# Layer 1 of a two-layer convolution kernel: one product for three taps, row shifts by DMA, and normalisation moved to ScalarE

## The chip, the cores and the metric

The kernel runs on one core of one Trainium2 chip. The metric is the device time of one execution in microseconds (us), lower is better. All data is float32. The engines are TensorE (PE in the profile, with PEld for its weight loads), VectorE (DVE), ScalarE (ACT), GpSimd (POOL) and SyncE (SP), which only issues DMAs here.

## The reference, cut to what matters

The input x has 2 images of 128 channels, 256 rows and 256 columns. Layer 0 is a group norm, a windowed attention with halo and a residual sum; its result goes to memory. The change concerns layer 1 (a further group norm `_gn` and a residual sum stand around this function):

```python
t1 = conv(x, w1, padding=((2, 2), (0, 0)))                    # 128 -> 128 channels, 5 taps down the rows
t3 = conv(t1, w3, padding=((1, 1), (0, 0)), feature_group_count=c)   # 3 taps down the rows, each channel alone
xp = pad(x, 2 columns left and right)
t2 = stack([xp[..., 0:w], xp[..., 2:w + 2], xp[..., 4:w + 4]])  # three taps along a row, 2 columns apart
t4 = einsum('nckhw,ckg->nghw', t2, w4[:, :, 0, :])             # 128 channels x 3 taps -> 8 channels
t5 = t4[:, None] * t3.reshape(n, c // g, g, h, w)              # the 8 channels multiply all 16 groups of t3
```

The output is `x + t5`, with x the input of the layer. The "unfolded products" are t4.

## The kernel before, in words

Channels lie on the 128 partitions. Both layers go through an image in strips of 8 rows, 32 strips per image, 64 strips in all. Layer 0 (`attention_fast`) writes its result x1 to memory; layer 1 (`convolutions_fast`) reads it back, 8 rows at a time, and a function per step issues the instructions. The order on each engine is the order in which the code calls these functions (`manual_schedule` over all five engines): an engine never takes a later instruction first.

One strip k of layer 1 in the order of the loop:

- `load_rows1(k + 2)`, L636 and L638: two DMAs of SP bring the rows of the strip after next into `raw` (six buffers).
- `unfold(k)`, L692: 12 matmuls into the PSUM tile `g`: for each of 3 taps, one for each of 4 pairs of rows. The weight is 128 x 32, its 8 real columns padded with zeros to 32; row pair j goes to PSUM partitions 32j to 32j + 31. ScalarE copies `g` to `t4` (L698).
- `first_rows(k)`, L723: ScalarE copies two rows of the vertical convolution from the strip before.
- `start_strip(k + 1)`, which is `normalise1`: ScalarE copies four rows of `xm` (the normalised input `xn`) from the strip before (L649), then VectorE subtracts the mean and multiplies by `rstd`, 128 x 2048 elements (L651).
- `vertical(k, 2)`: the 5-tap convolution for four rows, in PSUM tiles `a_c`, `a_d`, `a_e`, `a_o` (L706 and L740), in this order on TensorE, taken in turn from three buffers. ScalarE copies `a_c` to `both` (L737); VectorE forms `c` (L744) and the even and odd rows of `t1` (L751, L757); ScalarE starts `t3` (L762).
- `row_sums(k + 1)`: ScalarE copies one row of `sm` (L677), VectorE forms sums and differences of rows, `sm` and `df` (L678, L682), for the next strip.
- `depthwise(k, 2)`: VectorE, two instructions on `t3` (L769). Then `vertical(k, 4)` for the other four rows.
- `spread(k)`, L780: four matmuls with the selection matrix `sel` copy the 8 channels of `t4` to all 128 partitions, into the PSUM tiles `b`. `combine` multiplies them by `t3` (L789), with `depthwise(k, 4)` between its halves.
- `finish(k)`: a GpSimd DMA adds x1 from memory to `y` (L797), then an SP DMA writes `y` out (L798).

Group-norm values come from `Norms.steps`, whose small instructions are spread over several strips.

Of the kernel before, what the change touches and what calls it, by code (L numbers as in the profile page):

```python
# [9 lines left out]
F32 = mybir.dt.float32  # L10
I32 = mybir.dt.int32
AF = mybir.ActivationFunctionType
# [33 lines left out]

def host_constants():
    ident = np.eye(P, dtype=np.float32)  # L50
    gavg = np.zeros((P, P), np.float32)
    for g in range(P // 4):
        gavg[4 * g : 4 * g + 4, 4 * g : 4 * g + 4] = 0.25

    kb = np.zeros((HEADS, 32, 6, 10), np.float32)
    for c in range(10):
        kb[:, c, :, c] = 1.0
    for r in range(6):
        kb[:, 10 + r, r, :] = 1.0
    kb[:, 16, :, 6:] = NEG  # L60
    kb[:, 17, :, :4] = NEG
    flag = np.zeros((2, 4 * NPAIR * 4, 2, 4), np.float32)
    flag[0, :, 0] = 1.0
    flag[1, :, 1] = 1.0


    hot = np.zeros((2, HEADS, 16, 2, 64), np.float32)
    for key in range(64):
        j, i = divmod(key, 6)
        for e in range(2):  # L70
            if 0 <= j - 4 * e < 6:
                hot[:, :, j - 4 * e, e, key] = 1.0
            else:
                hot[:, :, 12, e, key] = NEG
            if key < 60:
                hot[:, :, 6 + i, e, key] = 1.0


    keep = np.zeros((2, HEADS, 16, 2, 2), np.float32)
    for i in range(2):  # L80
        keep[:, i::2, 0:12, i, 0] = 1.0
        keep[:, i::2, 12, i, 1] = 1.0

    sel = np.zeros((4, 32, P), np.float32)
    for ch in range(P):
        sel[:, ch % 8, ch] = 1.0
    return {
        "c_ident": ident,
        "c_sel": sel.reshape(P, P),
        "c_gavg": gavg,  # L90
        "c_kb": kb.reshape(P, 60),
        "c_flag": flag.reshape(2, 4 * NPAIR, 32),
        "c_hot": hot.reshape(P, 128),
        "c_keep": keep.reshape(P, 4),
        "c_head": np.stack([(np.arange(P) // DH % 2 == i) for i in range(2)], 1).astype(np.float32),
    }


class Norms:
# [15 lines left out]
    def steps(self, st, ps_pool, name, tag="pj"):  # L115

        nc, glob, small, gavg = self.nc, self.glob, self.small, self.gavg
        mv = small.tile([P, 2], F32, tag="mv", name=f"mv_{name}")
        nc.vector.bn_aggr(mv, st.rearrange("p n k -> p (n k)"))
        yield  # L120
        pm = ps_pool.tile([P, 512], F32, tag=tag, name=f"pm_{name}")
        nc.tensor.matmul(pm[:, 0:1], gavg, mv[:, 0:1], start=True, stop=True)
        yield
        mean = glob.tile([P, 1], F32, tag=f"mean_{name}", name=f"mean_{name}")
        nc.vector.tensor_copy(mean, pm[:, 0:1])
        d = small.tile([P, 1], F32, tag="d", name=f"d_{name}")
        nc.vector.tensor_sub(d, mv[:, 0:1], mean)
        q = small.tile([P, 1], F32, tag="q", name=f"q_{name}")
        nc.vector.tensor_mul(q, d, d)
        nc.vector.tensor_add(q, q, mv[:, 1:2])  # L130
        yield
        pv = ps_pool.tile([P, 512], F32, tag=tag, name=f"pv_{name}")
        nc.tensor.matmul(pv[:, 0:1], gavg, q, start=True, stop=True)
        yield
        v = small.tile([P, 1], F32, tag="v", name=f"v_{name}")
        nc.vector.tensor_scalar(v, pv[:, 0:1], 1e-5, None, ALU.add)
        yield
        sd = small.tile([P, 1], F32, tag="sd", name=f"sd_{name}")
        nc.scalar.activation(sd, v, AF.Sqrt)
        yield  # L140

        r0 = small.tile([P, 1], F32, tag="r0", name=f"r0_{name}")
        nc.vector.reciprocal(r0, sd)
        nc.vector.tensor_mul(r0, r0, v)
        nc.vector.tensor_add(r0, r0, sd)
        nc.vector.tensor_scalar(r0, r0, 0.5, None, ALU.mult)
        rstd = glob.tile([P, 1], F32, tag=f"rstd_{name}", name=f"rstd_{name}")
        nc.vector.reciprocal(rstd, r0)
        self.done[name] = mean, rstd
        yield  # L150

    def group(self, st, ps_pool, name):
        for _ in self.steps(st, ps_pool, name):
            pass
        return self.done[name]


def attention_fast(tc, io, x1_d, norm, st_x, st_y, tags, ends, weights):
# [6 lines left out]
    with ExitStack() as l0:  # L165
# [120 lines left out]
        def normalise(k):  # L286
            b, s = divmod(k, NS)
            if s == 0:
                norms[b] = norm.group(st_x[b], ps_pj, f"x{b}") if b == 0 else norm.done[f"x{b}"]
                st_y[b] = norm.new(f"st_y{b}", tags[(2 * b + 2) % 3])  # L290
                if b + 1 < NB:
                    st_x[b + 1] = norm.new(f"st_x{b + 1}", tags[(2 * b + 1) % 3])
# [290 lines left out]
class Weights:  # L583


    def __init__(self, nc, io, glob):
        self.nc, self.io = nc, io
        self.w1 = glob.tile([P, 5, P], F32, tag="w1", name="w1")
        self.w3 = glob.tile([P, 3], F32, tag="w3", name="w3")
        self.w4 = glob.tile([P, 3, 32], F32, tag="w4", name="w4")  # L590
        self.sel = glob.tile([P, P], F32, tag="sel", name="sel")
        self.w1s = glob.tile([P, 6, P], F32, tag="w1s", name="w1s")

# [13 lines left out]
def convolutions_fast(tc, io, x1_d, norm, st_y, out, weights, count_good):  # L607
# [4 lines left out]
    with ExitStack() as l1:  # L612
# [25 lines left out]
                nc.sync.dma_start(t[:, 5:8, :], x1_d[b][s + 1][:, 0:3, :])  # L638
            raws[b, s] = t

        def normalise1(b, s, k, mean, rstd):
            cur, prev = xn[k % 2], xn[(k + 1) % 2]
            if s == 0:
                nc.gpsimd.memset(cur[:, 0:1, :], 0.0)
                nc.vector.tensor_scalar(
                    cur[:, 1:4, 2 : 2 + W], raws[b, -1][:, 5:8, :], mean, rstd, ALU.subtract, ALU.mult
                )
            else:
                nc.scalar.copy(cur[:, 0:4, :], prev[:, 8:12, :])  # L649
            n = 8 if s + 1 < NS else 5  # L650
            nc.vector.tensor_scalar(  # L651
                cur[:, 4 : 4 + n, 2 : 2 + W], raws[b, s][:, 0:n, :], mean, rstd, ALU.subtract, ALU.mult
            )
            if n < 8:
                nc.gpsimd.memset(cur[:, 4 + n : 12, :], 0.0)

        t1s, sms, dfs = {}, {}, {}

# [25 lines left out]
        def unfold(k):  # L686

            xt = xn[k % 2]
            pg = ps_pj.tile([P, 512], F32, tag="pj", name=f"g_{k}")
            for tap in range(3):  # L690
                for j in range(4):
                    nc.tensor.matmul(  # L692
                        pg[32 * j : 32 * j + 32, :], w4[:, tap, :],
                        xt[:, 2 * j + 1 : 2 * j + 3, 2 * tap : 2 * tap + W],
                        start=tap == 0, stop=tap == 2,
                    )
            t4 = wk.tile([P, 512], F32, tag="t4", name=f"t4_{k}")
            nc.scalar.copy(t4, pg)  # L698
            t3 = wk.tile([P, 8, W], F32, tag="t3", name=f"t3_{k}")
            y = wk.tile([P, 8, W], F32, tag="y", name=f"y_{k}")  # L700
            ts[k] = t4, t3, y
# [22 lines left out]
            if s + 1 == NS:  # L724
                nc.gpsimd.memset(t1[:, 9:10, :], 0.0)

        def vertical(k, m):

            s = k % NS
            xt, sm, df, t1 = xn[k % 2], sms[k], dfs[k], t1s[k]  # L730
# [4 lines left out]
            pa = taps(f"{k}_c_{m}", 1, [(w1s[:, 0], sm[:, m - 1 : m])])  # L735
            both = wk.tile([P, 1, W], F32, tag="both", name=f"both_{k}_{m}")
            nc.scalar.copy(both, pa)  # L737
            pa = ps_a.tile([P, 512], F32, tag="a", name=f"a_{k}_d_{m}")
            for i, w in enumerate((w1[:, 1], w1s[:, 1])):
                nc.tensor.matmul(  # L740
# [33 lines left out]
        def spread(k):  # L774

            t4 = ts[k][0]
            banks = []
            for j in range(4):
                pb = ps_b.tile([P, 512], F32, tag=f"b{j}", name=f"b_{k}_{j}")
                nc.tensor.matmul(  # L780
                    pb, sel[32 * j : 32 * j + 32, :], t4[32 * j : 32 * j + 32, :], start=True, stop=True
                )
                banks.append(pb)
            return banks
# [9 lines left out]
        def finish(k):  # L794
            b, s = divmod(k, NS)
            t4, t3, y = ts.pop(k)
            nc.gpsimd.dma_start(y, x1_d[b][s], accum_op=ALU.add)  # L797
            nc.sync.dma_start(out[b, :, 8 * s : 8 * s + 8, :], y)  # L798
            del raws[b, s - 1]

        def finish_half(k, half):

# [11 lines left out]
        with tc.manual_schedule(engines=ORDERED):  # L814
# [4 lines left out]
            for k in range(NB * NS):  # L819
# [2 lines left out]
                    load_rows1(*divmod(k + 2, NS))  # L822
                unfold(k)
                first_rows(k)
                if more:
                    start_strip(k + 1)

                vertical(k, 2)


                if k in (1, 2):
# [6 lines left out]
                    row_sums(k + 1)  # L838
                depthwise(k, 2)
                vertical(k, 4)  # L840
                banks = spread(k)
                combine(k, banks, (0, 1))
                if not more:
# [566 lines left out]
def lay_out(inputs):  # L1410
# [4 lines left out]
        [np.asarray(inputs["L0_conv_rel_width"]).T, np.asarray(inputs["L0_conv_rel_height"]).T], axis=1  # L1415
    )
    w4 = np.asarray(inputs["L1_conv_w4"])[:, :, 0, :]
    return {
        "x": c(np.asarray(inputs["x"])),
        "w_qkvT": c(w_qkv.T),  # L1420
# [3 lines left out]
        "w1T": c(np.asarray(inputs["L1_conv_w1"])[:, :, :, 0].transpose(1, 2, 0)),  # L1424
        "w3": c(np.asarray(inputs["L1_conv_w3"])[:, 0, :, 0]),
        "w4": c(np.tile(w4, (1, 1, P // w4.shape[-1]))),
        "w4g": c(np.pad(w4, ((0, 0), (0, 0), (0, 32 - w4.shape[-1])))),
        **host_constants(),
    }

# [16 lines left out]
```

## Time and profile before

| | before |
|---|---|
| time, median of 3 runs (lowest to highest) | 3217.13 us (3214.41 to 3219.65) |
| the profiled execution: its time, its span | 3215.36 us, 3213.6 us |
| mean granted TensorE clock | 0.996 |
| layer 1 begins (first matmul of `g`) | 2104 us |
| TensorE / VectorE / ScalarE busy in 100 us of layer 1 (2400 to 2500) | 100.00 / 88.95 / 31.22 us |
| mean busy share of the 16 DMA engines there | 0.70 |

The span runs from the first to the last instruction of the core; the 1.8 us between it and the time lie around it. A timeline line has the start and the length in us, the engine, the source line, the operation, what it writes and reads, the shape and how many instructions are merged (x). A float32 matmul has two records, so 12 matmuls are x24. In square brackets stands the engine's idle time before the instruction and what ended it. `SPq` and `POOLq` are the queues that issue DMAs. In the list of DMA issues the last number is the median time from issue to landing.

### The profile page before, as it was taken

What the parts mean: (1) busy time and instruction counts of PE and PEld (TensorE: products, weight loads), DVE (VectorE), ACT (ScalarE), POOL (GpSimd) and SP (SyncE); (2) the same over time, 40 slices, a digit from 0 to 9 for tenths busy, and PEclk for the clock granted to TensorE, in tenths of its full rate; (3) what the DMA queues carried; (4) which work ended last, traced back from release to release, by engine and by line L of the source; (5) the groups of instructions that cost most, each with busy time, mean ns of one, the idle gap of its engine ahead of it and who ended that gap; (6) DMA issues with size and microseconds to landing.
All of it is one profiled execution on the core that took longest, in us unless ns stands there. A gap on an engine that the chain in (4) does not pass through costs nothing.

```text
span 3213.6 us, 117425 instructions
## 1 busy us (share of the span) xinstructions
PE 3081.7 (96%) x53030; PEld 2280.1 (71%) x53030; DVE 2611.1 (81%) x4152; ACT 1439.9 (45%) x2481; POOL 584.8 (18%) x917
## 2 busy tenths in 40 slices
PE   0799999999999999999999999989999999999998
PEld 0688998899998889999889998844444444444443
DVE  8788888888888777777777777679888898888887
ACT  0455555555555555555555555522332333233322
POOL 2222222222222222222222222100000000000001
PEclk9999999999999999999999999999999999999999
DMA  9433333333332222222222222146777676777775
GB/s 396 149 132 112 122 109 111 108 118 121 111 111 92 85 69 92 81 72 85 69 92 81 72 85 69 56 130 170 190 190 189 180 189 190 184 183 187 193 184 153
DMA packets 125116, 426.42 MB, mean 133 GB/s; under 512 B 9024, under 2 KB 75328, under 8 KB 92096
## 3 DMA queue, kind: packets, MB, share of 16 engines
q1 hardware_dynamic: 115536, 352.76, 32.2%
q0 software_dynamic: 9072, 66.06, 11.3%
q8 instruction: 420, 6.88, 0.9%
q14 instruction: 88, 0.72, 0.1%
HBM read 284.57 MB, written 134.22 MB: 130 GB/s over the span
## 4 chain that ended last, share of the span: by engine, by line
PE 85%; issue 10%; DVE 2%; DMA 1%; POOL 1%; ACT 0%; SPq 0%; POOLq 0%; DVEq 0%; ACTq 0%
PE f_pv L416 15%; PE f_pq L341 8%; PE f_s L451 8%; PE f_o L476 8%; PE a_e L706 7%; PE a_o L706 7%; PE f_pk L341 7%; PE f_py L341 7%; PE f_pa L395 4%; PE f_s L435 4%; PE g L692 4%; PE a_d L740 3%; PE b L780 2%; PE a_c L706 1%; DMA raw<-f_x 1%
## 5 line engine op out<-in xcount | busy, mean ns | idle before, releaser
L422 DVE COPY f_vt<-f_pv 64x512 f32<-64x512 f32 x512 | 354.4, 694 | 292.2 <-ACT f_vt L422 292.0
L416 PE MATMUL f_pv<-f_wqkvT,f_xn 128*128 128x128 f32 x4096 | 491.3, 278 | 0.0
L416 PEld LDWEIGHTS f_pv<-f_wqkvT,f_xn 128*128 128x128 f32 x4096 | 466.9, 192 | 8.6
L762 ACT ACTIVATE t<-t,w 128x1024 f32<-128x1024 f32 x128 | 147.3, 1151 | 687.2 <-DVE t L757 666.8
L323 POOL COPY f_xq<-f_xn 128x256 f32<-128x256 f32 x512 | 310.6, 651 | 756.1 <-DVE f_xn L309 756.1
L376 ACT ACTIVATE f_q<-f_pq,f_head 128x512 f32<-128x512 f32 x512 | 310.2, 688 | 303.4 <-PE f_pq L341 303.4
L460 ACT ACTIVATE f_p<-f_s 128x512 f32<-128x512 f32 x512 | 264.3, 602 | 404.2 <-PE f_s L451 404.2
L422 ACT COPY f_vt<-f_pv 64x512 f32<-64x512 f32 x512 | 297.3, 582 | 118.1 <-PE f_pv L416 117.9
L769 DVE SCALAR_TENSOR_TENSOR t<-t,w,t 128x1024 f32<-128x1024 f32 x256 | 329.9, 1289 | 7.6 <-ACT t L762 1.3
L451 PEld LDWEIGHTS f_s<-f_q,f_kt 64*64 64x64 f32 x16384 | 250.6, 135 | 49.2 <-issue 49.2
L341 PE MATMUL f_pq<-f_xn,f_wq_s 128*128 128x192 f32 (+2 forms) x1520 | 277.1, 329 | 3.3 <-DVE f_xn L309 2.5
L451 PE MATMUL f_s<-f_q,f_kt 64*64 64x64 f32 x16384 | 268.1, 220 | 0.0
L476 PE MATMUL f_o<-f_vt,f_p 128*32 128x66 f32 x16384 | 264.4, 222 | 1.1 <-issue 0.4
L797 POOL DMA_DIRECT2D y<-f_x x63 | 68.1, 1082 | 1017.5 <-DVE y L789 1003.5
L476 PEld LDWEIGHTS f_o<-f_vt,f_p 128*32 128x32 f32 x16384 | 242.5, 110 | 10.6 <-DVE f_cf L408 1.0
L341 PE MATMUL f_pk<-f_xn,f_wqkvT 128*128 128x256 f32 x1024 | 245.2, 380 | 0.0
L341 PEld LDWEIGHTS f_pq<-f_xn,f_wq_s 128*128 128x128 f32 x1520 | 232.4, 188 | 16.9 <-issue 4.2
L341 PE MATMUL f_py<-f_ot,f_woT 128*128 128x256 f32 x1024 | 241.7, 378 | 2.3 <-DVE f_ot L494 2.3
L706 PE MATMUL a_o<-xm,w1s 128*128 128x512 f32 x512 | 240.5, 590 | 0.5 <-ACT both L737 0.5
L706 PE MATMUL a_e<-xm,w1s 128*128 128x512 f32 x512 | 240.7, 591 | 0.0
L300 POOL COPY f_xn<-f_xn 128x1280 f32<-128x1280 f32 x62 | 86.9, 1402 | 772.0 <-PE f_pv L416 772.0
L510 DVE TENSOR_TENSOR f_x<-f_py,f_raw 128x512 f32<-128x512 f32 x256 | 176.0, 688 | 58.1 <-PE f_py L341 50.3
(126 smaller groups left out, 4607.7 us busy)
## 6 DMA issues: line engine op xcount, KB each, us to landing
f_raw<-in_x SPq DMA_DIRECT2D x62, 1280.0 KB, 7.8
f_sx<-in_x SPq DMA_DIRECT2D x64, 1024.0 KB, 7.2
f_x<-f_x SPq DMA_DIRECT2D x128, 512.0 KB, 3.3
y<-f_x POOLq DMA_DIRECT2D x63, 1024.0 KB, 8.2
out<-y SPq DMA_DIRECT2D x63, 1024.0 KB, 4.9
raw<-f_x SPq DMA_DIRECT2D x64, 640.0 KB, 6.4
raw<-f_x SPq DMA_DIRECT2D x62, 384.0 KB, 6.9
f_raw<-in_x SPq DMA_DIRECT2D x2, 1024.0 KB, 7.1
```

What stands on the lines that cost most here:

```text
L323: nc.gpsimd.tensor_copy(xq[:, t2, half].rearrange("p t r n c e -> p r t (n c) e"), cells[:, :, 16 * half : 16 * half + 16, 1 + t2 : 9 : 4, ...
L341: nc.tensor.matmul(dst[:, 32 * lo : 32 * hi], w, moving[:, lo:hi], start=True, stop=True)
L376: nc.scalar.activation(q[:, c, :, i], pq.rearrange("p (n x) -> p n x", n=NPAIR), AF.Copy, scale=head[:, i : i + 1],)
L416: nc.tensor.matmul(pv[:, P * n : P * n + P], xn[k % 2][:, r, 4 * j + n].rearrange("p c x -> p (c x)"), wvT, start=True, stop=True,)
L422: (nc.vector.tensor_copy if c else nc.scalar.copy)(vt[rows, 4 * j : 4 * j + 4, :, c, 0:32], pv[rows].rearrange("p (n h d) -> p n h d", n=4 ...
L451: nc.tensor.matmul(sc[g][n // 8][64 * c : 64 * c + 64, n % 8].rearrange("p i x -> p (i x)"), keys_k[rows, c, 48 * n : 48 * n + 64], qs[u][ ...
L460: nc.scalar.activation(pts[u][:, g, 8 * half : 8 * half + 8].rearrange("p n i x -> p (n i x)"), sc[g][half].rearrange("p n i x -> p (n i x ...
L476: nc.tensor.matmul(po[32 * h : 32 * h + 32, n - lo], p[:, h // 2, n, h % 2], vt[:, n, h], start=True, stop=True,)
L510: nc.vector.tensor_tensor(x1[:, :, c:W:2], py.rearrange("p (m t) -> p t m", t=4), raws[k][:, r:8:2, c:W:2], ALU.add,)
L706: nc.tensor.matmul(pa[:, : n * W], w, rows, start=i == 0, stop=i == len(terms) - 1)
L762: nc.scalar.activation(t3[:, j : j + 4], t1[:, j : j + 4, :], AF.Copy, scale=w3[:, 0:1])
L769: nc.vector.scalar_tensor_tensor(t3[:, j : j + 4], t1[:, j + tap : j + tap + 4, :], w3[:, tap : tap + 1], t3[:, j : j + 4], ALU.mult, ALU.add,
```

## The change

Four things are done together, all in layer 1:

1. `unfold` makes one matmul per row pair instead of three. The weight's 32 columns now hold the 8 columns of each tap side by side, in four slots of 8 of which one is a repeat (`SLOTS`), so one pass gives the products of all three taps at the unshifted column. ScalarE copies the result twice: into `plain`, which has two columns of zeros at either side, and into `t4`. Five SP DMAs then overwrite the partitions of the two outer taps in `t4` by rows of `plain` read two columns to the left or right. `sel` now has a 1 for each of the three slots, so `spread` sums the taps as it copies.
2. `normalise1` runs on ScalarE, in two passes over the 128 x 2048 elements: add the negative mean (`less`), then multiply by `rstd`.
3. `start_strip(k + 1)` is called inside `vertical(k, 2)`, after the copy to `both`.
4. The output DMA of a strip is issued one strip later, in `store(k - 1)`, ahead of `spread(k)`.

```diff
+SLOTS = ((3, 1, 0), (0, 1, 3), (3, 1, 0), (0, 1, 3))
...
-    sel = np.zeros((4, 32, P), np.float32)
-    for ch in range(P):
-        sel[:, ch % 8, ch] = 1.0
+    sel = np.zeros((4, 4, 8, P), np.float32)
+    for j in range(4):
+        for ch in range(P):
+            sel[j, SLOTS[j], ch % 8, ch] = 1.0
...
+        less = glob.tile([P, 1], F32, tag=f"less_{name}", name=f"less_{name}")
+        nc.vector.tensor_scalar(less, mean, -1.0, None, ALU.mult)
...
-            nc.vector.tensor_scalar(
-                cur[:, 4 : 4 + n, 2 : 2 + W], raws[b, s][:, 0:n, :], mean, rstd, ALU.subtract, ALU.mult
-            )
+            rows = cur[:, 4 : 4 + n, 2 : 2 + W]
+            nc.scalar.activation(rows, raws[b, s][:, 0:n, :], AF.Identity, bias=less)
+            nc.scalar.activation(rows, rows, AF.Copy, scale=rstd)
...
-            for tap in range(3):
-                for j in range(4):
-                    nc.tensor.matmul(
-                        pg[32 * j : 32 * j + 32, :], w4[:, tap, :],
-                        xt[:, 2 * j + 1 : 2 * j + 3, 2 * tap : 2 * tap + W],
-                        start=tap == 0, stop=tap == 2,
-                    )
-            t4 = wk.tile([P, 512], F32, tag="t4", name=f"t4_{k}")
-            nc.scalar.copy(t4, pg)
+            for j in range(4):
+                nc.tensor.matmul(
+                    pg[32 * j : 32 * j + 32, :], w4[:, j], xt[:, 2 * j + 1 : 2 * j + 3, 2 : 2 + W],
+                    start=True, stop=True,
+                )
+            plain = by_pixel[k % 2]
+            pixels = pg.rearrange("p (r w) -> p r w", w=W)
+            t4 = wk.tile([P, 2, W], F32, tag="t4", name=f"t4_{k}")
+            nc.scalar.copy(plain[:, :, 2 : 2 + W], pixels)
+            nc.scalar.copy(t4, pixels)
+
+            for lo, hi, o in ((24, 40, 0), (88, 104, 0), (0, 8, 4), (56, 72, 4), (120, 128, 4)):
+                nc.sync.dma_start(t4[lo:hi], plain[lo:hi, :, o : o + W])
...
             nc.scalar.copy(both, pa)
+            if between:
+                between()
...
             nc.gpsimd.dma_start(y, x1_d[b][s], accum_op=ALU.add)
-            nc.sync.dma_start(out[b, :, 8 * s : 8 * s + 8, :], y)
+            done[k] = y
...
+        def store(k):
+            b, s = divmod(k, NS)
+            nc.sync.dma_start(out[b, :, 8 * s : 8 * s + 8, :], done.pop(k))
...
-                if more:
-                    start_strip(k + 1)
-
-                vertical(k, 2)
+
+                vertical(k, 2, (lambda: start_strip(k + 1)) if more else None)
...
                 vertical(k, 4)
+                if k > 0:
+
+                    store(k - 1)
                 banks = spread(k)
```

More of the change, by code (lines that the diff above doesn't have):

```diff
@@ L148, in steps @@
         nc.vector.reciprocal(rstd, r0)
-        self.done[name] = mean, rstd
+        less = glob.tile([P, 1], F32, tag=f"less_{name}", name=f"less_{name}")
+        nc.vector.tensor_scalar(less, mean, -1.0, None, ALU.mult)
+        self.done[name] = mean, rstd, less
         yield
@@ L154, in group @@
             pass
-        return self.done[name]
+        return self.done[name][:2]
 def attention_fast(tc, io, x1_d, norm, st_x, st_y, tags, ends, weights):
@@ L288, in normalise @@
             if s == 0:
-                norms[b] = norm.group(st_x[b], ps_pj, f"x{b}") if b == 0 else norm.done[f"x{b}"]
+                norms[b] = norm.group(st_x[b], ps_pj, f"x{b}") if b == 0 else norm.done[f"x{b}"][:2]
                 st_y[b] = norm.new(f"st_y{b}", tags[(2 * b + 2) % 3])
@@ L589, in __init__ @@
         self.w3 = glob.tile([P, 3], F32, tag="w3", name="w3")
-        self.w4 = glob.tile([P, 3, 32], F32, tag="w4", name="w4")
+        self.w4 = glob.tile([P, 4, 32], F32, tag="w4", name="w4")
         self.sel = glob.tile([P, P], F32, tag="sel", name="sel")
@@ L639, in load_rows1, with normalise1 @@
             raws[b, s] = t
-        def normalise1(b, s, k, mean, rstd):
+        def normalise1(b, s, k, mean, rstd, less):
             cur, prev = xn[k % 2], xn[(k + 1) % 2]
@@ L657, in convolutions_fast @@
         t1s, sms, dfs = {}, {}, {}
+        done = {}
+        by_pixel = [cst.tile([P, 2, W + 4], F32, tag=f"t4{i}", name=f"t4p_{i}") for i in range(2)]
+        for i in range(2):
+            for side in (0, 2 + W):
+                nc.gpsimd.memset(by_pixel[i][:, :, side : side + 2], 0.0)
         def start_strip(k):
@@ L725, in first_rows, with vertical @@
                 nc.gpsimd.memset(t1[:, 9:10, :], 0.0)
-        def vertical(k, m):
+        def vertical(k, m, between=None):
             s = k % NS
@@ L780, in spread @@
                 nc.tensor.matmul(
-                    pb, sel[32 * j : 32 * j + 32, :], t4[32 * j : 32 * j + 32, :], start=True, stop=True
+                    pb, sel[32 * j : 32 * j + 32, :],
+                    t4[32 * j : 32 * j + 32].rearrange("p r w -> p (r w)"), start=True, stop=True,
                 )
@@ L1417, in lay_out @@
     w4 = np.asarray(inputs["L1_conv_w4"])[:, :, 0, :]
+    w4g = np.zeros((P, 4, 4, 8), np.float32)
+    for j in range(4):
+        w4g[:, j, SLOTS[j]] = w4
     return {
@@ L1426, in lay_out @@
         "w4": c(np.tile(w4, (1, 1, P // w4.shape[-1]))),
-        "w4g": c(np.pad(w4, ((0, 0), (0, 0), (0, 32 - w4.shape[-1])))),
+        "w4g": c(w4g),
         **host_constants(),
```

## The prediction

> **What bounds the kernel now.** The page's engine shares come first, then the table of stretches for layer 1, then the timeline of one undisturbed strip there, engine by engine.
>
> ```profile
> PE 3081.7 (96%) x53030; PEld 2280.1 (71%) x53030; DVE 2611.1 (81%) x4152; ACT 1439.9 (45%) x2481; POOL 584.8 (18%) x917
> ```
>
> ```profile
> core 0: us, PE busy (x) PEld busy (x) DVE busy (x) ACT busy (x) POOL busy (x), PEclk, DMA share, GB/s
> 2400.00:2500.00 100.00, 100.00 (x407) 45.52 (x406) 88.95 (x102) 31.22 (x48) 6.62 (x6) 1.00 0.70 187
> ```
>
> In layer 1 TensorE has no gap, VectorE is busy 89%, ScalarE 31%. A busy PE alone proves little, so the timelines must show who waits for whom:
>
> ```profile
> 2809.68 1.14 PE L780 MATMUL b<-t,sel 32*128 32x512 f32 x8
> 2810.75 2.80 PE L692 MATMUL g<-xm,w 128*32 128x512 f32 x24
> 2813.48 0.70 PE L706 MATMUL a_c<-sm,w1s 128*128 128x256 f32 x2
> ...
> 2827.64 2.79 PE L692 MATMUL g<-xm,w 128*32 128x512 f32 x24
> ```
>
> ```profile
> 2811.21 0.13 PEld L692 LDWEIGHTS g<-xm,w 128*32 128x32 f32 x4 [0.30 <-issue]
> 2811.64 0.13 PEld L692 LDWEIGHTS g<-xm,w 128*32 128x32 f32 x4 [0.30 <-issue]
> ```
>
> ```profile
> 2816.45 1.34 DVE L651 TENSOR_SCALAR xm<-raw,mean_y,rstd_y 128x2048 f32<-128x2048 f32 x1
> ...
> 2820.23 0.69 DVE L757 TENSOR_TENSOR t<-a_o,c 128x512 f32<-128x512 f32 x1 [1.05 <-PE a_o L706]
> 2820.84 1.22 DVE L678 TENSOR_TENSOR sm<-xm 128x1024 f32<-128x1024 f32 x1
> 2822.49 1.23 DVE L682 TENSOR_TENSOR df<-sm 128x1024 f32<-128x1024 f32 x1 [0.44 <-ACT sm L677]
> ```
>
> ```profile
> 2813.61 0.59 ACT L698 COPY t<-g 128x512 f32<-128x512 f32 x1 [1.12 <-PE g L692]
> ...
> 2814.62 1.06 ACT L649 COPY xm<-xm 128x1040 f32<-128x1040 f32 x1
> 2815.58 0.37 ACT L737 COPY both<-a_c 128x256 f32<-128x256 f32 x1
> 2821.02 1.15 ACT L762 ACTIVATE t<-t,w 128x1024 f32<-128x1024 f32 x1 [5.07 <-DVE t L757]
> ```
>
> A strip takes 2827.64 - 2810.75 = 16.89 us. VectorE waits 1.05 us for TensorE each strip (L757) and 0.44 us for ScalarE; TensorE waits for no one. So **TensorE's issue of matmuls bounds layer 1**, and VectorE is close behind. `g` holds TensorE for 2813.48 - 2810.75 = 2.73 us. Its weight loads come in fours, 0.43 us apart: the four row pairs run side by side, so 12 matmuls are 6 such rounds, 6 x 0.43 = 2.58, plus 0.15 at the edges.
>
> ```profile
> 2807.55 0.34 SPq L798 DMA_DIRECT2D out<-y  x1
> 2807.94 0.43 SPq L636 DMA_DIRECT2D raw<-f_x  x1
> 2808.41 0.90 SPq L638 DMA_DIRECT2D raw<-f_x  x1
> ```
>
> ```profile
> y<-f_x POOLq DMA_DIRECT2D x63, 1024.0 KB, 8.2
> out<-y SPq DMA_DIRECT2D x63, 1024.0 KB, 4.9
> raw<-f_x SPq DMA_DIRECT2D x64, 640.0 KB, 6.4
> raw<-f_x SPq DMA_DIRECT2D x62, 384.0 KB, 6.9
> ```
>
> SP waits for the adding DMA (L797) before it may issue the output, and the loads queue behind: they come just in time (the waits list has 15.4 us of VectorE waiting for `raw`).
>
> **What the Trainium skill says.** "TensorEngine Tiling (Array Packing)", Key Properties: column tiles of one array run in parallel, and a change of tiling mode drains it. The trace agrees (fours every 0.43 us, 0.15 us at the edges). "ScalarE: Activation LUTs", What ACT_TABLE_LOAD costs, and its section on table sets: an ACTIVATE with a per-partition operand takes about 280 ns + 0.833 ns per element, neighbours overlap by 93 ns, and identity and copy are in every set. L762 agrees (1133 ns by that rule, 1151 measured), and so do Identity and Exp, which alternate in layer 0 (three table loads ahead of 512 Exps). "DMA: Bandwidth & Descriptors", Queues, rings and completion order: an engine consumes one ring in order, so small DMAs of SP stand behind large ones of SP. No run shown yet tests that.
>
> **The change part by part.** Zero is the start of `g` in strip k.
>
> *TensorE.* 8 of 12 matmuls go: 4 of 6 rounds, 4 x 0.43 = **1.72 us less per strip**; `g` becomes 1.01 us. Bounds: 0.86 (no edge) and 1.07 (`b`, also one round of four matmuls, 2809.68 to 2810.75). The period becomes 15.17 us if TensorE stays the bound. `spread` keeps its four matmuls but must wait for five more DMAs; I take 0.05 us of semaphore handling (from 0, where it hides behind the matmuls in flight, to 0.3; VectorE's semaphore instructions take 0.02 us each).
>
> *ScalarE.* All else here moves 1.72 us earlier with `g`: the first copy starts at 2813.61 - 2810.75 - 1.72 = 1.14. Then `plain` (to 1.6), `t4` (an extra 0.59, less overlap: 0.49; done at 2.2), L723 (to 2.6), `both` (now ahead of the normalisation, to 2.9), the four-row copy (to 3.9), two passes. The trace has no such pass: by the skill 280 + 0.833 x 2048 = 1.99 us each, and the groups' 1060 ns for L649 (1040 elements) against 623 for L723 (512) give 0.83 ns per element, so 1.90 us without an operand. I take 1.99; less than 1.9 is excluded by that slope, above I allow 2.4. With 1.99 they end at **7.8**. ScalarE's busy time rises from 5.2 by 0.5 + 3.9 to 9.6 of 15.17 us. Queued behind the passes are L762, the `sm` copy and the second `both`. L762 waits for L757 anyway, which starts at 2820.23 - 2810.75 - 1.72 = 7.76 and feeds it 0.79 later, at 8.55. So the passes fit, in the 5.07 us idle slot above, by 0.75.
>
> *VectorE.* It loses L651, 1.34, of 15.0 us per strip. L678 now needs ScalarE's second pass (7.8, and about 0.1 for the semaphore) and would start at 8.37: cover 0.5 us. VectorE's slack at L757 was 1.05; it gains 1.34 and the period shrinks by 1.72, so 0.67 us is left. Hence TensorE still bounds. The buffers in turn: matmuls of `a_e` in the second half reuse the first `a_o`, freed by L757 at 8.45 and needed at 10.57 - 1.72 = 8.85, the same 0.4 us as before. The second `a_o` needs the second `both`, ready near 10.2, at about 11.4.
>
> *DMAs.* Order on SP: loads (k + 2), five shifts (k), output (k - 1). Small SP loads at the kernel's start took 0.43 us to issue and 1.9 to 2.6 to land. The shifts wait for `t4` (2.2): issued until 2.3 + 5 x 0.47 = 4.7, landed by 7 on an empty ring. It isn't empty: the adding DMA starts at 6.1 in strip k - 1 (2816.83 - 2810.75 now) and lands 8.2 later at 14.3, which is -0.9 here; output and loads follow, the last landing 0.86 + 6.9 = 7.8 after the output's issue, at 6.9. Behind them the shifts land at about **7 to 10**; `spread` needs them at 15.17 - 1.07 = 14.1. Cover: 4 us. They add 64 partitions x 2 KB = 128 KB to 3 MB per strip; DMA share 0.70 x 16.89/15.17 + about 0.02 = 0.80. GpSimd's queue is passed by nothing. A late output holds only `y`, which is next written at 15.7 of strip k + 1, over 10 us after landing. The loads are now issued a strip ahead of need: VectorE's 15 us of waits go, worth 0 since TensorE wasn't held.
>
> *Ends.* In strip 0 the raw rows land at 2107.6; normalising then takes 3.9 instead of 1.35 us on the path, which eats that strip's gain: 0. `less` is three tiny VectorE instructions: 0. The tail follows TensorE: gains as the others.
>
> **Sum.** 63 x (1.72 - 0.05) = 105 us. Against the profiled execution: 3215.36 - 105 = 3110; the median stands 1.77 above it: **3112 us**. Ends of the unknowns: `g` at 0.86 and no semaphore cost give -118 (3099); `g` at 1.07 and 0.3 give -86 (3132).
>
> **Rivals.**
> - *ScalarE/VectorE become the bound* (0.14). If the two passes exceed 1.99 each by more than 0.25 to 0.3, L678 and L762 slip, and after another 0.67 us the period grows. At 2.8 us each the slip is 1.6 - 0.5 - 0.67 = 0.4 us per strip, 27 us: 3139; at 3.0, +0.8, 3164. For it: covers of half a microsecond. Against: L762's and L649's durations are steady within 0.01 us.
> - *The shifts hold `spread`* (0.04, slower than before). Place: PE's wait ahead of L780. SP is one ordered queue, so a late adding DMA delays the output, the loads, the shifts, `spread`, and with `combine` the next adding DMA. It decides if the shifts land after 14.1 and loses all gain after 15.8, 6 us later than I think; at 17.1, 3.0 - 1.72 = +1.3 us per strip: 3299. For it: DMAs of both kinds nearly fill the strip (8.2 + 7.8 of 16.89 us). Against: 4 us of cover, and the DMA engines idle 20%.
> - *It doesn't do what it says*: four matmuls with different weights don't run side by side (0.02). Then one round costs 4 x 0.86, about 3.5 us, 0.8 above today: 3267. Against: `g` and `b` overlap now, with separate weight loads per tile.
>
> **How the numbers follow.** TensorE-bound with the gain kept: 0.78, own range 3099 to 3132. The measurement can tell about 0.2%, 6 us, from no change. Faster by more: 0.78 + 0.14 and none of the others, 0.92; same 0.02, for cases between; slower 0.04 + 0.02 = 0.06. The range 3099 to 3150 takes half of the first rival.
>
> **What would show it.** After: `g` as x8 over about 1.0 us; strips of about 15.2 us; PE still near 100% in layer 1; ScalarE about 64%, VectorE about 90%; L757 still waiting for `a_o`, about 0.7 us; no wait of TensorE for `t4`'s DMAs ahead of `b`. Wrong if `b` waits for DMAs, if L678 waits for ScalarE's pass for long, or if the passes take over 2.3 us.

## The result, and the profile after

The changed kernel takes 3107.26 us (median of 4 runs, 3106.21 to 3108.70) against 3216.56 us of the kernel before (median of 4): a ratio of 0.966, 95% interval 0.9643 to 0.9677, or 109.3 us less. The prediction was 3112 us. The profiled execution took 3106.21 us, its span 3104.3 us.

The page's engine shares and one row of the table of stretches in layer 1 (columns: stretch; its length; busy us of PE, PEld, DVE, ACT, POOL with instruction counts; clock; DMA share; GB/s):

```profile
PE 2971.1 (96%) x52006; PEld 2248.5 (72%) x52006; DVE 2533.3 (82%) x4092; ACT 1711.4 (55%) x2673; POOL 569.0 (18%) x921
```

```profile
2400.00:2500.00 100.00, 100.00 (x348) 47.03 (x347) 91.37 (x106) 60.35 (x73) 5.18 (x6) 1.00 0.81 216
```

TensorE still has no gap in this stretch; ScalarE has nearly doubled, from 31% to 60%. TensorE's timeline of a strip:

```profile
2511.07 1.14 PE L799 MATMUL b<-t,sel 32*128 32x512 f32 x8
2512.14 1.07 PE L704 MATMUL g<-xm,w 128*32 128x512 f32 x8
2513.14 0.70 PE L723 MATMUL a_c<-sm,w1s 128*128 128x256 f32 x2
...
2527.30 1.08 PE L704 MATMUL g<-xm,w 128*32 128x512 f32 x8
```

`g` is x8 instead of x24 and holds TensorE for 2513.14 - 2512.14 = 1.00 us, where it was 2.73. (Its weight is still 32 columns wide: three slots of 8 hold the taps, and the fourth holds zeros, not the repeat that the list of changes speaks of.) The strip takes 15.16 us, where it was 16.89. Over the 62 strips from the second `g` to the last (2129.08 to 3074.98, before 2128.75 to 3182.52) that makes 945.90 us against 1053.77, or 1.74 us less per strip. These 107.9 us are nearly the whole gain of 109.3; the rest lies behind the last `g`, where that strip is shorter too. Layer 0 is as before to within 0.6 us.

ScalarE's timeline of the same strip, with the lines that matter later:

```profile
2512.70 1.15 ACT L781 ACTIVATE t<-t,w 128x1024 f32<-128x1024 f32 x1 [5.53 <-DVE t L776]
2513.75 0.57 ACT L711 COPY t4p<-g 128x512 f32<-128x512 f32 x1
...
2516.44 2.02 ACT L660 ACTIVATE xm<-raw,less_y 128x2048 f32<-128x2048 f32 x1
2518.49 2.01 ACT L661 ACTIVATE xm<-xm,rstd_y 128x2048 f32<-128x2048 f32 x1
2520.62 1.15 ACT L781 ACTIVATE t<-t,w 128x1024 f32<-128x1024 f32 x1
2521.68 0.39 ACT L690 COPY sm<-sm 128x256 f32<-128x256 f32 x1
```

The two passes (L660, L661) fill the idle time in which ScalarE used to wait for VectorE. From L711 to the second L781 it has no idle time worth a bracket. VectorE at the same place:

```profile
2519.89 0.69 DVE L776 TENSOR_TENSOR t<-a_o,c 128x512 f32<-128x512 f32 x1 [0.62 <-PE a_o L723]
2520.53 1.23 DVE L691 TENSOR_TENSOR sm<-xm 128x1024 f32<-128x1024 f32 x1
2522.09 1.23 DVE L695 TENSOR_TENSOR df<-sm 128x1024 f32<-128x1024 f32 x1 [0.34 <-ACT sm L690]
```

VectorE still waits 0.62 us for TensorE: TensorE is the bound. But the pass ends at 2518.49 + 2.01 = 2520.50 and the sums that need it start at 2520.53, directly behind.

The step from the start of L661 to that of `t3` is 2520.62 - 2518.49 = 2.13 us; the 0.12 us between the end of the one and the start of the other matter below.

The queue of SP, and the landing times from the page's list of DMA issues:

```profile
2510.92 0.33 SPq L823 DMA_DIRECT2D out<-y  x1
2511.30 0.43 SPq L644 DMA_DIRECT2D raw<-f_x  x1
2511.77 0.92 SPq L646 DMA_DIRECT2D raw<-f_x  x1
2514.83 3.43 SPq L715 DMA_DIRECT2D t<-t4p  x5
```

```profile
out<-y SPq DMA_DIRECT2D x63, 1024.0 KB, 4.0
...
t<-t4p SPq DMA_DIRECT2D x192, 32.0 KB, 4.3
```

The five shifts (L715) are issued in 3.43 us. In this stretch they took 4.2 us to land (3.9 to 5.1), so the last, issued near 2517.6, is there by about 2522 to 2523; `b` needs them at 2526.23.

### The profile page after: what moved, and what is told of

Read it like the earlier page. It is cut to its first block, busy times and chain, and to the rows that moved or that the text cites. A ratio compares the mean times of both kernels' runs of the same rounds, so it can differ in the third digit from the quotient of the medians.

```text
span 3104.3 us, 116029 instructions
## 1 busy us (share of the span) xinstructions
PE 2971.1 (96%) x52006; PEld 2248.5 (72%) x52006; DVE 2533.3 (82%) x4092; ACT 1711.4 (55%) x2673; POOL 569.0 (18%) x921
## 4 chain that ended last, share of the span: by engine, by line
PE 92%; DVE 2%; issue 1%; DMA 1%; ACT 0%; POOL 0%; SPq 0%; DVEq 0%; POOLq 0%; ACTq 0%
PE f_pv L424 15%; PE a_e L723 10%; PE a_o L723 10%; PE f_pq L349 9%; PE f_s L459 8%; PE f_o L484 8%; PE f_pk L349 7%; PE f_py L349 7%; PE f_pa L403 4%; PE f_s L443 4%; PE a_d L759 3%; PE b L799 2%; PE a_c L723 2%; PE g L704 2%; DVE t L788 0%
## 5 line engine op out<-in xcount | busy, mean ns | idle before, releaser
L781 ACT ACTIVATE t<-t,w 128x1024 f32<-128x1024 f32 x128 | 147.0, 1149 | 375.2 <-DVE t L776 369.5
L817 POOL DMA_DIRECT2D y<-f_x x63 | 54.5, 866 | 925.1 <-DVE y L809 910.1
```

The lines of the kernel that those rows point to most:

```text
L781: nc.scalar.activation(t3[:, j : j + 4], t1[:, j : j + 4, :], AF.Copy, scale=w3[:, 0:1])
```

## The experiments

The theory: TensorE's issue bounds layer 1, the gain is the two rounds of four matmuls taken out, and all else the change does only keeps other chains under the new, shorter strip. (A round is here four matmuls side by side, 0.86 us; it is two of the rounds of 0.43 us that the prediction counts.) The rivals: VectorE's relief brings part of the gain; the shifts cost something; a chain through ScalarE or SP's queue is nearer to the bound than the prediction said. Where a result is compared with 3107 us, the kernel before took 3216.4 to 3218.0 us beside it.

**One more round of `g`.**

```diff
-            for j in range(4):
-                nc.tensor.matmul(pg[32 * j : ...], w4[:, j], ...)
+            for again in range(2):
+                for j in range(4):
+                    nc.tensor.matmul(pg[32 * j : ...], w4[:, j], ...)
```

> The changed kernel with the four matmuls of `g` issued twice, the second overwriting the first with the same values. Theory: one more round of four costs 0.86 us of TensorE per strip, 64 x 0.86 = 55 us: 3162 us (3157 to 3167). Rival (TensorE's issue is not the bound, or matmuls hide under something): 3107 to 3120.

Measured: 3160.8 us, +53.5, or 0.84 us for each of 64 strips. In TensorE's timeline `g` grew from 1.00 to 1.87 us:

```profile
2613.63 1.94 PE L705 MATMUL g<-xm,w 128*32 128x512 f32 x16
2615.50 0.70 PE L724 MATMUL a_c<-sm,w1s 128*128 128x256 f32 x2
```

So a round costs the time what it holds TensorE, to within 0.03 us per strip.

**The move to ScalarE alone, on the kernel before.** The normalisation and its place as in the change; 12 matmuls, no shifts, stores as before.

```diff
-            nc.vector.tensor_scalar(cur[...], raws[b, s][...], mean, rstd, ALU.subtract, ALU.mult)
+            nc.scalar.activation(rows, raws[b, s][:, 0:n, :], AF.Identity, bias=less)
+            nc.scalar.activation(rows, rows, AF.Copy, scale=rstd)
...
-                if more:
-                    start_strip(k + 1)
-                vertical(k, 2)
+                vertical(k, 2, (lambda: start_strip(k + 1)) if more else None)
```

> The kernel before, with only the normalisation moved to ScalarE in two passes and called after the copy to `both`; the 12 matmuls of `g` stay, no shifts, stores as before. Theory: TensorE still issues 16.89 us of matmuls per strip, so 3216 us within 6; VectorE's wait for `a_o` grows from 1.05 to about 2.3 us. Rival (VectorE's relief or the lost waits for loads are part of the gain): 3190 or less.

Measured: 3216.06 us, ratio 0.9994 (0.9985 to 1.0002). VectorE's busy share in layer 1 fell from 89% to 82%, and the time stayed:

```profile
2500.00:2600.00 100.00, 100.00 (x404) 45.14 (x403) 82.09 (x96) 54.16 (x60) 5.17 (x6) 1.00 0.71 187
```

```profile
2614.94 0.69 DVE L755 TENSOR_TENSOR t<-a_e,c 128x512 f32<-128x512 f32 x1 [0.56 <-PE a_e L708]
2617.52 0.69 DVE L761 TENSOR_TENSOR t<-a_o,c 128x512 f32<-128x512 f32 x1 [1.88 <-PE a_o L708]
```

VectorE's wait for TensorE grew from 1.05 to 2.44 us, in two pieces instead of the one of 2.3 that was expected. By itself the relief is worth nothing.

**The change without the move.**

```diff
-            nc.scalar.activation(rows, raws[b, s][:, 0:n, :], AF.Identity, bias=less)
-            nc.scalar.activation(rows, rows, AF.Copy, scale=rstd)
+            nc.vector.tensor_scalar(rows, raws[b, s][:, 0:n, :], mean, rstd, ALU.subtract, ALU.mult)
```

> The changed kernel with the normalisation back on VectorE in one pass, at the same place in the order. Theory (TensorE bounds at 15.16 us per strip, and VectorE had only 0.62 us of slack there): VectorE's chain grows from 13.80 us busy plus 0.34 and 0.40 of waits and gaps by 1.25 to 15.9 us, so it becomes the bound, +0.7 us per strip, about 3107 + 46 = 3153 us (3140 to 3165). Rival (fewer matmuls do it all, the move to ScalarE is worth nothing): 3107. Rival (the move is what brought the gain): near 3216.

Measured: 3145.16 us, ratio 0.9779 (0.9762 to 0.9795), so 38 us of the 109 go. VectorE's timeline no longer has a wait for TensorE at the additions; a stretch of 100 us shows it at 94%:

```profile
2500.00:2600.00 100.00, 98.77 (x324) 44.03 (x323) 94.36 (x109) 33.83 (x55) 8.09 (x8) 1.00 0.79 207
```

```profile
2517.43 1.34 DVE L660 TENSOR_SCALAR xm<-raw,mean_y,rstd_y 128x2048 f32<-128x2048 f32 x1
2518.68 0.68 DVE L762 TENSOR_TENSOR c<-a_d,both 128x512 f32<-128x512 f32 x1
2519.47 0.69 DVE L769 TENSOR_TENSOR t<-a_e,c 128x512 f32<-128x512 f32 x1
2520.08 0.68 DVE L775 TENSOR_TENSOR t<-a_o,c 128x512 f32<-128x512 f32 x1
```

The strip is 15.78 us (`g` at 2511.73 and 2527.51), VectorE's own chain with its waits for ScalarE. The terms expected add up to 13.80 + 0.34 + 0.40 + 1.25 = 15.79, not to the 15.9 written there; with 15.79 the same forecast is +0.63 us per strip, about 40 us in 63 strips. Alone the move brings no time, as the run before shows, but without it 38 of the 109 us are lost.

**No shifts.**

```diff
-            for lo, hi, o in ((24, 40, 0), (88, 104, 0), (0, 8, 4), (56, 72, 4), (120, 128, 4)):
-                nc.sync.dma_start(t4[lo:hi], plain[lo:hi, :, o : o + W])
```

> The changed kernel without the five shift DMAs, so the two outer taps are read at the middle column (this part of the computation is changed). Theory: they land several us before `spread` needs them, so 3107 us within 5. Rival (their issue on SP, their traffic or TensorE's waits for them cost something): lower by more than 6 us.

Measured: 3106.59 us (3106.14 to 3108.42, where the changed kernel takes 3106.21 to 3108.70). No cost of the shifts, of their issue or of TensorE's waits for them can be seen.

**The output not deferred.**

```diff
             nc.gpsimd.dma_start(y, x1_d[b][s], accum_op=ALU.add)
-            done[k] = y
+            nc.sync.dma_start(out[b, :, 8 * s : 8 * s + 8, :], y)
...
-                if k > 0:
-                    store(k - 1)
```

> The changed kernel with the output DMA issued by SP at the end of its own strip, as in the kernel before, instead of one strip later. Theory: SP is one ordered queue, so the shifts of strip k + 1 now wait for the adding DMA of strip k; that closes a loop through `spread`, `combine`, the adding DMA (8 us), the output's and loads' issue, the shifts (3.4 us of issue and 4.3 to land) and `spread` again, about 26 us per strip, so 3600 to 3850 us, with TensorE waiting ahead of `b`. Rival (the deferral is a detail, SP's order is covered): 3107 within 15.

Measured: 3666.64 us, ratio 1.14 (1.1375 to 1.142). The timelines of SP, GpSimd and TensorE, in this order, walk the loop:

```profile
2605.46 0.34 SPq L818 DMA_DIRECT2D out<-y  x1
...
2607.34 3.72 SPq L715 DMA_DIRECT2D t<-t4p  x5
2629.54 0.34 SPq L818 DMA_DIRECT2D out<-y  x1
```

```profile
2621.59 0.86 POOL L817 DMA_DIRECT2D y<-f_x  x1 [23.23 <-DVE y L809]
```

```profile
2605.84 1.02 PE L723 MATMUL a_o<-xm,w 128*128 128x512 f32 x2
2614.02 2.40 PE L799 MATMUL b<-t,sel 32*128 32x512 f32 x8 [7.16 <-DMA t<-t4p]
...
2638.04 2.38 PE L799 MATMUL b<-t,sel 32*128 32x512 f32 x8 [5.53 <-DMA t<-t4p]
```

SP issues the output at 2605.46, then the loads, and can issue the shifts only from 2607.34; `b` gets them at 2614.02, `combine` frees the adding DMA at 2621.59, and 7.95 us later, at 2629.54, SP is let go. One turn took 24.0 us (2614.02 to 2638.04), where about 26 was expected. So the fourth item of the change, which looks like a detail, is what lets the first pay with the shifts on SP. Shifts issued by another engine were not tried.

**ScalarE with less and with more work.** One pass (scale and bias at once), a third pass over all elements, over half, and over an eighth:

```diff
-            nc.scalar.activation(rows, raws[b, s][:, 0:n, :], AF.Identity, bias=less)
-            nc.scalar.activation(rows, rows, AF.Copy, scale=rstd)
+            nc.scalar.activation(rows, raws[b, s][:, 0:n, :], AF.Identity, bias=less, scale=rstd)
```

(`less` then holds the negative mean times `rstd`.)

> The changed kernel with the normalisation in one ScalarE pass (scale rstd, bias -mean x rstd). Theory: ScalarE loses 2.05 us per strip that TensorE never waited for: 3107 us within 5. Rival (ScalarE's chain, which ends just in time for the sums on VectorE, already holds the strip): lower by 10 us or more.

Measured: 3105.47 us, ratio 0.9654 (0.9637 to 0.967): not to be told from the changed kernel's.

```diff
+            nc.scalar.activation(rows, rows, AF.Copy)
```

> The changed kernel with a third ScalarE pass, a copy of the 128 x 2048 elements onto themselves. Theory: the passes end with next to no cover ahead of the sums and of `t3`; the slip of about 1.95 us eats VectorE's slack of 0.62 and the rest shows: +1.3 us per strip, 3107 + 80 = 3187 us (3165 to 3200). Rival (ScalarE is idle 38% of the strip, so a pass of 2 us is hidden): 3107 to 3112.

Measured: 3209.98 us, +103, nearly the whole gain, and outside the range expected (3165 to 3200).

```diff
+            nc.scalar.activation(cur[:, 4:8, 2 : 2 + W], cur[:, 4:8, 2 : 2 + W], AF.Copy)
```

> The same with an extra pass over half of the elements, 128 x 1024. Theory: a slip of about 1.0 us less the slack of 0.62: +0.4 us per strip, about 3107 + 25 = 3132 us (3120 to 3140). Rival (idle ScalarE hides it): 3107 to 3112. Rival (no slack on VectorE at all): 3107 + 63 = 3170.

Measured: 3157.86 us, +51, twice what the theory gave. It took VectorE's slack of 0.62 us as cover; VectorE's timeline of this run shows that it never was:

```profile
2513.80 0.68 DVE L777 TENSOR_TENSOR t<-a_o,c 128x512 f32<-128x512 f32 x1
2516.24 1.23 DVE L692 TENSOR_TENSOR sm<-xm 128x1024 f32<-128x1024 f32 x1 [1.76 <-ACT xm L662]
2517.58 1.23 DVE L696 TENSOR_TENSOR df<-sm 128x1024 f32<-128x1024 f32 x1
```

VectorE now runs its additions early (L777 waits for no one) and stands 1.76 us before L692 instead. ScalarE's timeline of the same strip, from one `t3` of the second half to the next:

```profile
2507.31 1.15 ACT L782 ACTIVATE t<-t,w 128x1024 f32<-128x1024 f32 x1 [5.54 <-DVE t L777]
...
2513.10 2.01 ACT L661 ACTIVATE xm<-xm,rstd_y 128x2048 f32<-128x2048 f32 x1
2515.15 1.06 ACT L662 ACTIVATE xm<-xm 128x1024 f32<-128x1024 f32 x1
2516.12 1.13 ACT L782 ACTIVATE t<-t,w 128x1024 f32<-128x1024 f32 x1
2517.16 0.39 ACT L691 COPY sm<-sm 128x256 f32<-128x256 f32 x1
...
2523.35 1.15 ACT L782 ACTIVATE t<-t,w 128x1024 f32<-128x1024 f32 x1 [5.54 <-DVE t L777]
```

The chain that holds the strip leaves out TensorE and most of VectorE's slack: ScalarE's `t3` of the second half, its copies, the passes, `t3` of the first half, the `sm` copy; then on VectorE `df`, `depthwise`, three additions, which release ScalarE's `t3` again. In this run a turn is 16.04 us (2507.31 to 2523.35). The extra pass puts the step from the start of L661 to that of `t3` at 2.05 + 0.97 us, where 2.01 - 0.09 = 1.92 would do without it (0.09 is by how much L662 and `t3` overlap here): 1.10 us. So in the changed kernel the loop takes 14.94 us, only 0.23 below TensorE's 15.17. Two other places agree. In the changed kernel's own timeline that step is 2.13 us, so 0.21 more than the 1.92 that would do. And with the whole third pass it is 2.04 + 1.82 us (L661, L662 and `t3` start at 2516.24, 2518.28 and 2520.10), which gives a loop of 14.94 + 3.86 - 1.92 = 16.88 us; `g` came every 16.89 there (2525.70 to 2542.59). Two more runs test the number with forecasts made ahead.

```diff
+            nc.scalar.activation(cur[:, 4:5, 2 : 2 + W], cur[:, 4:5, 2 : 2 + W], AF.Copy)
```

> The changed kernel with a small extra ScalarE pass over 128 x 256 of the elements after the two. New theory (a loop from `t3` of the second half on ScalarE through the copies, the two passes, `t3`, the `sm` copy, then `df`, `depthwise` and three additions on VectorE back to that `t3` takes 16.04 - 1.10 = 14.94 us, so only 0.23 us below TensorE's 15.17): the pass adds 2.05 + 0.28 - 1.92 = 0.41 us to the loop, +0.18 per strip, 3107 + 11 = 3118 us (3113 to 3123). Old theory (cover plus VectorE's slack of 0.62 us): 3107 within 4.

Measured: 3120.12 us, ratio 0.9696 (0.9683 to 0.9709): +13. `g` now comes every 15.39 us, 0.22 more than TensorE's 15.17, where 0.18 was forecast:

```profile
2506.34 1.08 PE L705 MATMUL g<-xm,w 128*32 128x512 f32 x8
...
2521.73 1.07 PE L705 MATMUL g<-xm,w 128*32 128x512 f32 x8
```

The loop stands; the cover of 0.62 is refuted.

```diff
-            nc.scalar.activation(rows, rows, AF.Copy, scale=rstd)
+            nc.scalar.activation(cur[:, 4:8, 2 : 2 + W], cur[:, 4:8, 2 : 2 + W], AF.Copy)
```

(with scale and bias in the first pass, as above)

> The changed kernel with one ScalarE pass (scale and bias at once) and the extra pass over 128 x 1024 that cost 50 us behind two passes. New theory: the loop is 2.05 us shorter by the pass left out, so 14.94 - 2.05 + 1.10 = 14.0 us, and the extra pass costs nothing: 3107 us within 4. Rival (an extra ScalarE pass delays whatever its place in a loop, about 0.8 us per strip): near 3157.

Measured: 3107.34 us. Behind one pass the same extra work that cost 51 us costs nothing, and VectorE waits for TensorE again as in the changed kernel:

```profile
2507.92 0.69 DVE L776 TENSOR_TENSOR t<-a_o,c 128x512 f32<-128x512 f32 x1 [0.62 <-PE a_o L723]
```

One pass therefore leaves more room, though it is no faster. No version here beats the changed kernel beyond the scatter of the runs.

## Why the prediction was right, point by point

- *The bound and the gain.* Right. `g` at 1.00 us (1.01 predicted), strip 15.16 (15.17), 1.74 us per strip over the steady part (1.72). The extra round shows the price to be TensorE's time. The four matmuls with their different weights do run side by side, so the third rival is out.
- *TensorE's handling of five more waits.* 0.05 us per strip was taken; leaving the shifts out changes nothing that can be measured, so it is near 0, the lower end. This term, 3 us, is the larger part of the 5 us by which the forecast was high.
- *VectorE.* Slack 0.67 predicted, 0.62 seen as the wait for `a_o`; that it would be the bound without the move is shown (15.78 us).
- *ScalarE.* Here two terms were mis-sized. The first copy was put at 1.14 us after `g`'s start; it started at 1.61, because `t3` of the second half stands ahead of it and is released by VectorE's additions, no longer hidden behind a 2.73 us `g`. The passes were put at 3.9 us together; they took 2518.49 + 2.01 - 2516.44 = 4.06, since the second did not overlap the first, whose output it reads. (The Trainium skill, "ScalarE: Activation LUTs", What ACT_TABLE_LOAD costs, gives 1.99 us for one and an overlap of 93 ns between neighbours. The measured lengths, 2.02 and 2.01, agree. The overlap doesn't hold for this dependent pair, which has a gap of 0.03; the extra passes behind L661 show gaps of 0.02 to 0.04.) The passes ended at 8.36, not 7.8.
- *The first rival's threshold.* This step failed: "and after another 0.67 us the period grows". VectorE's slack is no cover for a loop that runs through ScalarE and enters VectorE behind the waiting addition. The cover was 0.23 us in all. By the loop, passes of 2.8 us, which the prediction priced at +0.4 us per strip, would cost about 14.94 + 2 x 2.8 - 4.03 - 15.17 = 1.3 (an estimate; 4.03 is the length of the two passes). TensorE still won, but by that margin and not by the half microsecond and more that was named, and nothing in the prediction had found how thin it was: to this extent the right number was luck.
- *The shifts.* Predicted to land 7 to 10 us after `g`; the last lands at about 9.7 to 10.6, against 14.1 needed. Each took 0.61 us to issue (median) where the small loads at the kernel's start, on which the prediction built, took 0.43. SP as one ordered queue was the second rival; without the deferred output it is real and costs 559 us against the changed kernel. What that run shows is the order in which SP issues: it waited 18.6 us per strip for the adding DMA (1077.3 us in 58 waits), and the loads and shifts stood behind. The Trainium skill, "DMA: Bandwidth & Descriptors", Queues, rings and completion order, speaks of a later step, the order in which a DMA engine takes the entries of its ring; no run here separates the two.
- *The ends.* The first strip was put at no gain. The second `g` starts at 2129.08 where it was 2128.75, although layer 1's first matmul came 0.6 us earlier (2103.43 against 2104.07): the first strip lost about a microsecond, within what the sum can tell. `less` is four VectorE instructions of 0.13 us, not three; put at nothing, they don't show.

## What to carry to other kernels

Price a removed matmul by the rounds that it holds TensorE, then walk each other engine's order as a loop from an instruction back to itself, since slack that one engine shows at one wait isn't cover for a chain that enters behind that wait. When small DMAs with a near deadline join an ordered queue, look first for the entry ahead of them that waits for something late, and move that one. Adding to the suspected work in steps (an eighth, a half, the whole) measures a margin that no single wait in the profile shows.

## What was not expected of the hardware

In the run without the deferred output, `b` took 2.40 us and the following `g` 1.94, against 1.14 and 1.07 without idle time ahead. The slow stretch ends with the first `a_e`, which has its usual length:

```profile
2616.35 1.94 PE L704 MATMUL g<-xm,w 128*32 128x512 f32 x8
2618.22 1.22 PE L723 MATMUL a_c<-sm,w1s 128*128 128x256 f32 x2
...
2620.74 1.02 PE L723 MATMUL a_e<-xm,w 128*128 128x512 f32 x2
```

The clock column read 0.85 over 100 us there, instead of 1.00; from 2614.0 to 2620.5 it read 0.50. The Trainium skill, "TensorE: Matmul & The Clock Gate", Part 1, says that after an idle window of about 3.4 us the array runs at half its clock until it has been busy for such a window. The waits of 7.16 and 5.53 us and the 0.50 agree; the way back took longer here, about 6.5 us of work. From the start of `b` to that of the first `a_e` TensorE needed 6.72 us (2614.02 to 2620.74) where the changed kernel needs 3.47 (2511.07 to 2514.54). So a wait of that length costs TensorE more than itself, here about 3.3 us per strip. Little of it lengthened this run's loop: from the start of `b` to the adding DMA it took 7.57 us, against 7.11 in the changed kernel (2511.07 to 2518.18).
